# Two attention blocks on one core: the first block's output projection by a two-level product scheme, and who forms its factors

## The chip, the cores and the metric

One core of a Trainium2 chip runs the whole program. The metric is the time on the device in microseconds, as the median of several runs. All data is 32-bit floating point (`F32`).

## What is computed

The input holds B = 8 images of C = 512 channels and 32 x 32 = 1024 positions (tokens). Two attention blocks follow each other. The first has 32 normalisation groups and 8 heads:

```python
h = group_norm(x, gn_weight, gn_bias)
qkv = jnp.einsum('oc,bct->bot', w_qkv, h.reshape(B, C, T)) + b_qkv[None, :, None]
...
weight = jnp.einsum('bct,bcs->bts', q * scale, k * scale)
weight = jax.nn.softmax(weight.astype(jnp.float32), axis=-1).astype(weight.dtype)
a = jnp.einsum('bts,bcs->bct', weight, v)
out = jnp.einsum('oc,bct->bot', w_proj, a) + b_proj[None, :, None]
return x + out.reshape(B, C, H, W)
```

The second has 8 groups and one head over all 512 channels, with the same shape: normalisation, `q`, `k`, `v`, softmax, a projection, and the residual `x + ...`. This document is about the line `out = ...` and the residual behind it in the first block.

## The kernel before

**Images and stages.** A channel tile is 128 channels x 1024 tokens, so an image has four. The loop `for b in range(B)` (L1055 on) runs image b through the first block and image b - 1 through the second: attention of b (`attention0`), the projection of b (`projection`), then for image b - 1 the product `g` (`conv2("m", ...)`), the scores (`scores1`), the product `z` and the values (`values1`), and then `v`, `k` and `q` of image b + 1. The first image's start is in `prologue`. TensorE's instructions are kept in program order. So are VectorE's, GpSimd's and ScalarE's where the code says `tc.keep_in_program_order`; a scheduler places the others when the program is built. On the chip each engine takes its queue in order.

**Seven products in place of eight.** Every 512 x 512 by 512 x 1024 product is cut into halves each way, and formed with seven half-size products in place of eight (Strassen's scheme in Winograd's form). The seven left and seven right factors are the quarters themselves and sums of quarters. `image_factors` makes the right ones from four tiles: `t1 = b12 - b11`, `t2 = b22 - t1`, a new `b12 = b22 - b12`, and `t4 = b21 - t2` (two operations of 128 x 512 each, L1071 when pinned to VectorE). Factor 1 is b11, 2 is b21, 3 is b22, 4 is t4, 5 is t1, 6 is t2, 7 is the new b12.

**One level or two.** `by_channel` (through `wino`) stops there: 28 matmuls of 128 x 512. `conv2` does it twice: each of the seven factors is cut again by `inner_factors` (four subtractions of 128 x 256 for each factor, L414, on GpSimd), which gives 49 matmuls of 128 x 256. `conv2` takes the outer products in four parts (`pair`), one or two at a time, and goes through the seven inner products of a part in `inner_steps` in the order 1, 6, 2, 5, 7, with 3 and 4 left in `tail`, which the next part runs behind its product 1. After product 1 ScalarE copies its result to a second bank of PSUM, where 6, 7 and 4 go on. `add` (VectorE) and `nc.scalar.copy` bring results out; `more` (GpSimd, L535) adds one block of the output to another.

**Before, the projection uses `by_channel`** (L986), with the order `middle=(5, 6, 7, 2)`. VectorE's `residual` adds the projection's result and the bias `obias[0]` to `x` straight from PSUM (L964, L968, L970). The `x` tiles are loaded before the projection begins, and spilled behind it. The inner factors of `h`, which the next product `g` (or, in the first turn, `v`) reads, are 28 GpSimd operations in one run behind attention.

**Attention of the first block** goes through eight stretches of one pair of heads and half of the tokens. In a stretch ScalarE forms eight tiles of exponentials `e` (L651), VectorE adds them up (`sum`, L653 and L655), and TensorE multiplies them by `v` into `av`. Every two stretches (singly in the last two) `reciprocals` sums over partitions on TensorE (`sums`), copies the line to SBUF (L610), sends it through DRAM into 128 partitions, takes reciprocals (`recs`, L617) and spreads them back as `r`. The last stretch takes a short way: the reciprocal directly from PSUM (L607), and its DMAs from ScalarE's queue (L608, L628). Then `a` is scaled by `r` (L684). The lists `extra` put other work into the stretches: entry 2i + 1 of it comes behind the scaling in stretch i.

**SyncE's queue** issues nearly all loads in order. Weight factors are kept in DRAM (`keep`, or `keep2` with the second level) and loaded through three buffers in the order of the list `uses`. Image tiles and exponentials share one pool, `big`, of `NBIG` buffers of 4 KB in each partition.

Of the kernel before, what the change touches and what calls it, by code (L numbers as in the profile page):

```python
# [9 lines left out]
F32 = mybir.dt.float32  # L10
# [8 lines left out]
NBIG = 32  # L19
# [10 lines left out]
def two_attention_blocks_kernel(  # L30
# [22 lines left out]
    ident = const.tile([P, P], F32, name="ident")  # L53
    make_identity(nc, ident)
    ones = const.tile([P, P], F32, name="ones")
# [115 lines left out]
    def main_path(ctx):  # L171
# [100 lines left out]
        def weight_factors(t):  # L272
            return {p: t[:, ORDER.index(p), :, :] for p in range(1, 8)}

        def prepare(n):
            t = wpool.tile([P, 7, 2, C // 2], F32, tag="w", name=f"prepare_{n}")
            half = lambda kh, mh: weights[n][ts(kh, C // 2), ts(mh, C // 2)].rearrange("(k p) m -> p k m", p=P)
            f = weight_factors(t)
# [13 lines left out]
        wdram2 = {n: dram.tile([P, 7, 7, P], F32, name=f"sums2_{n}") for n in "qkmv"}  # L292
# [21 lines left out]
        uses = ["p", *layer0] if B > 1 else ["p"]  # L314
        for b in range(1, B):
            uses += ["p", *twice["m"], "z"] + (layer0 if b + 1 < B else [])
# [86 lines left out]
        def inner_factors(hf, uid, pin=lambda ins: ins):  # L403

            f, steps = {}, []
            for p in ORDER:
# [5 lines left out]
                def make(ops=((t1, b12, b11), (t2, b22, t1), (t3, b22, b12), (t4, b21, t2))):  # L412
                    for dst, x, y in ops:
                        pin(nc.gpsimd.tensor_tensor(dst, x, y, ALU.subtract))  # L414
# [86 lines left out]
        def conv2(n, f, bias, name, hooks=(), after=(), by_tokens=False):  # L501
# [30 lines left out]
            def more(dst, x, y, r, cc):  # L532

                (d,), (x,), (y,) = (blocks([at], r, cc) for at in (dst, x, y))
                nc.gpsimd.tensor_tensor(d, x, y, ALU.add)  # L535
# [8 lines left out]
            def pair(s, products, y, x, final):  # L544
# [6 lines left out]
                w = weights2[s // 2][:, (0, 2, 0, 1)[s] :]  # L551

                def mm(ps, j, start):
                    for i, p in enumerate(products):
                        wt = w[:, i, j - 1, :]
# [9 lines left out]
                def extra(r, cc, read, done):  # L565
                    if products == (7,):
                        if read:
                            more((0, 1), (0, 1), (1, 1), r, cc)
                        if done:
                            more((1, 1), (1, 0), (1, 1), r, cc)  # L570

# [6 lines left out]
            pair(0, (1, 5), [(1, 0), (1, 1)], None, [])  # L578
            pair(1, (2, 6), [(0, 0), (0, 1)], [(1, 0), (1, 0)], [load_weight, lambda: biased_half(0, 0)])
# [6 lines left out]
        def reciprocals(totals, uid, across, direct=None):  # L586
# [8 lines left out]
            for t in range(n):  # L595
                for i in range(4):
                    matmul(
                        sums[ts(i, 32), t, :, :], ones[:, :32], totals[t][:, :, ts(i, P)],
# [209 lines left out]

        def natural(wt, nm, banks):
# [3 lines left out]
            for kc in range(KC):  # L813
                for o in range(KC):
                    transpose(pt[o][:, ts(kc, P)], wt[kc][:, ts(o, P)], ident)
# [36 lines left out]
        def prologue():  # L852
            raw_k = raw("k", 5)
# [46 lines left out]
            for n in "pz":  # L900
                t, steps = prepare(n)
                later.append(steps)
                later.append([lambda n=n, t=t: keep(n, t), load_weight])
# [50 lines left out]
        def projection(b, af, xt, hooks=()):  # L954

            norm = GroupNorm(1, f"1_{b}", pinned=b > 0)
            stats, rest = [], []

            def residual(i, r, c, ps, u):
                oc = 2 * r + i  # L960
                xh = xt[oc][:, ts(c, HT)]

                tc.keep_in_program_order(
                    nc.vector.scalar_tensor_tensor(xh, ps, obias[0][:, oc : oc + 1], xh, ALU.add, ALU.add)  # L964
                )
                if (r, c) == (1, 1):

                    rest.append(lambda: tc.keep_in_program_order(nc.vector.tensor_add(xh, xh, u)))  # L968
                elif u is not None:
                    nc.vector.tensor_add(xh, xh, u)  # L970
                stats.append(lambda: norm.half_stats(oc, c, xh))

                if c == 1 - r:
                    stats.append(lambda: norm.end_stats(oc))

            def add_rest():
                for f in rest:
                    f()

            def store():  # L980
# [3 lines left out]

            by_channel(
                weight("p"), af, f"p_{b}", residual, middle=(5, 6, 7, 2), hooks=[[], [], hooks, [], [add_rest]],  # L986
                after=[load_weight, store],
            )
            return norm, stats
# [33 lines left out]
        def layer1_scores(b, inner):  # L1023
            g = conv2("m", inner, ubias, f"g1_{b}")
# [30 lines left out]
        for b in range(B):  # L1055
# [7 lines left out]
            elif B > 1:  # L1063
# [9 lines left out]

            if b > 0:
                hf, t = image_factors(h, f"h1_{b - 1}", here)
                for i, fs in enumerate((t[:1], t[1:2], (t[2], t[4]), (t[6], t[3]), (t[5], t[7]), steps[:2], steps[2:4])):
                    extra[2 * i + 3] += fs
            elif B > 1:
                hf, t = image_factors(h, "h0_1", here)
                for i, fs in enumerate((t[:2], (t[2], t[4]), (t[6], t[3]), (t[5], t[7], *steps[:2]), steps[2:4])):  # L1080
                    extra[2 * i + 7] += fs
            psum_pools(f"attention_{b}", 1)
            scaled = attention0(b, q, k, v, a, extra)
            if B > 1:
                for f in steps[4:7]:
                    f()
            psum_pools(f"products_{b}", 2)
            xt = [load_x(b, c, "x") for c in range(KC)]
            if B > 1:

                inner, sums2 = inner_factors(hf, f"h1_{b - 1}" if b > 0 else "h0_1", tc.keep_in_program_order)
                for f in sums2:
                    f()
                norm1, stats = projection(b, af, xt, [scaled, steps[7]])
# [235 lines left out]
```

## Time and profile before

| what | before |
|---|---|
| median of 3 runs (lowest, highest) | 2827.73 us (2827.01, 2831.14) |
| the profiled execution, its span on the core | 2828.69 us, 2826.9 us |
| granted TensorE clock, mean | 0.999 |
| DMA | 292.41 MB, 103 GB/s on average |
| projection's matmul records, `psa_p`, `psb_p`, `psc_p` | 448 of 128 x 512 |

PE is TensorE's matmul queue and PEld its weight loads; DVE is VectorE, ACT ScalarE, POOL GpSimd, SP SyncE, and a q behind a name is that engine's queue of DMA issues. A timeline line gives the start, the time from the start of its first to the end of its last instruction, the engine, the line of the code, the operation, output and inputs with their shape, and how many instructions it merges. In brackets it has the idle time of the engine just before, and what ended it. Durations overlap: the next instruction of an engine may start before the last has ended. Each 32-bit matmul shows as two records.

### The profile page before, as it was taken

The page shows a single profiled execution, that of the slowest core. Times are in us where ns is not written, and L with a number is a line of the kernel's source. Part 1 is how long each engine was busy: PE and PEld are TensorE (multiplying, and loading weights), DVE is VectorE, ACT ScalarE, POOL GpSimd, SP SyncE. Part 2 cuts the span into 40 slices and gives each one's busy share as a digit, 9 for nine tenths or more (in the row PEclk, how much of TensorE's full clock was granted, in tenths as well). Part 3 has the DMA queues.
Part 4 walks back from the last instruction along what each step waited for, and adds up shares of the span by engine and source line. Part 5 has one row for each costly group of instructions (what it writes and reads, how often), then busy time and mean ns, then how long its engine had stood idle before and what let it go on. Part 6 is the DMA issues. An engine that isn't in the chain of part 4 may idle for free.

```text
span 2826.9 us, 33696 instructions
## 1 busy us (share of the span) xinstructions
PE 2808.6 (99%) x12434; PEld 1693.5 (60%) x12434; DVE 2005.0 (71%) x2833; ACT 942.7 (33%) x1205; POOL 1099.4 (39%) x1131
## 2 busy tenths in 40 slices
PE   9999999999999999999999999999999999999998
PEld 5435735866367653677537674376843868338584
DVE  5478677776777767777677766777667776676765
ACT  1252452214522145221552215422154312633130
POOL 2204205841057410664107730177202672036672
PEclk9999999999999999999999999999999999999999
DMA  8634303043031330323212232123311224112301
GB/s 285 209 114 151 147 17 127 27 174 139 24 139 52 147 129 17 139 98 120 110 50 105 101 138 90 53 102 122 140 67 53 102 112 159 36 58 90 119 5 72
DMA packets 107344, 292.41 MB, mean 103 GB/s; under 512 B 19171, under 2 KB 51235, under 8 KB 97446
## 3 DMA queue, kind: packets, MB, share of 16 engines
q1 hardware_dynamic: 105382, 287.92, 28.8%
q10 hardware_dynamic: 1792, 2.29, 0.3%
q8 instruction: 100, 1.64, 0.2%
q14 instruction: 70, 0.57, 0.1%
HBM read 237.47 MB, written 52.70 MB: 103 GB/s over the span
## 4 chain that ended last, share of the span: by engine, by line
PE 96%; DVE 2%; issue 1%; DMA 0%; POOL 0%; ACT 0%; DVEq 0%; ACTq 0%; POOLq 0%
PE sc L62 16%; PE av L62 15%; PE psb_av L62 6%; PE psb L62 5%; PE psa_av L62 4%; PE psc_av L62 4%; PE psc L62 3%; PE psa L62 3%; PE psb_z L62 3%; PE psb_k L62 3%; PE psb_g L62 3%; PE psb_v L62 3%; PE psb_p L62 3%; PE psb_q L62 2%; PE psa_z L62 2%; PE psc_z L62 2%
## 5 line engine op out<-in xcount | busy, mean ns | idle before, releaser
L655 DVE TENSOR_TENSOR sum<-sum,e 128x1024 f32<-128x1024 f32 x384 | 483.9, 1260 | 37.4 <-ACT e L651 0.5
L651 ACT ACTIVATE e<-sc 128x1024 f32<-128x1024 f32 x512 | 476.0, 1054 | 75.8 <-PE sc L62 74.2
L62 PE MATMUL sc<-q,k 64*128 64x512 f32 x2048 | 456.8, 596 | 0.0
L62 PE MATMUL av<-e,v 128*64 128x512 f32 x2048 | 453.6, 595 | 0.0
L684 POOL TENSOR_TENSOR a<-a,r 128x512 f32<-128x512 f32 (+1 forms) x11 | 20.0, 1817 | 903.3 <-DMA r<-all_rows 771.0
L62 PEld LDWEIGHTS sc<-q,k 64*128 64x128 f32 x2048 | 191.6, 186 | 248.0 <-issue 110.6
L62 PEld LDWEIGHTS av<-e,v 128*64 128x64 f32 x2048 | 141.3, 137 | 304.4 <-issue 292.3
L653 DVE TENSOR_TENSOR sum<-e,e 128x1024 f32<-128x1024 f32 x64 | 78.4, 1225 | 166.5 <-ACT e L651 166.5
L669 ACT COPY a<-av 128x512 f32<-128x512 f32 x64 | 37.5, 586 | 321.9 <-PE av L62 321.9
L62 PE MATMUL psb<-inner,inner_h 128*128 128x256 f32 x448 | 116.1, 382 | 0.9
L62 PE MATMUL psa_av<-e,z 128*128 128x512 f32 x256 | 113.3, 595 | 0.0
L414 POOL TENSOR_TENSOR inner_h<-h,inner_h 128x256 f32<-128x256 f32 x120 | 111.6, 931 | 3.5
L135 ACT ACTIVATE h<-h,b,s 128x1024 f32<-128x1024 f32 x62 | 78.5, 1270 | 87.1 <-DMA h<-in_x 69.4
L414 POOL TENSOR_TENSOR inner_h<-h 128x256 f32<-128x256 f32 x60 | 64.6, 1076 | 83.6 <-ACT h L135 83.6
L62 PEld LDWEIGHTS psb<-inner,inner_h 128*128 128x128 f32 x448 | 83.9, 190 | 16.6 <-POOL inner L429 3.5
L462 ACT COPY psb_v<-psa_v 128x512 f32<-128x512 f32 (+1 forms) x28 | 14.5, 517 | 222.4 <-DVE o L785 141.5
L725 POOL TENSOR_TENSOR sum<-sum,e 128x1024 f32<-128x1024 f32 x32 | 76.1, 2378 | 27.4 <-ACT e L721 26.1
L62 PE MATMUL psb_g<-inner_h,w_m 128*128 128x256 f32 x336 | 86.0, 383 | 0.3
L414 POOL TENSOR_TENSOR inner_h<-t_h,inner_h 128x256 f32<-128x256 f32 x90 | 84.2, 935 | 2.4
L414 POOL TENSOR_TENSOR inner_h<-t_h 128x256 f32<-128x256 f32 x90 | 79.9, 894 | 9.7 <-DVE t_h L165 9.7
L62 PEld LDWEIGHTS psa_av<-e,z 128*128 128x128 f32 x256 | 48.0, 190 | 57.3 <-issue 56.6
L721 ACT ACTIVATE e<-e 128x1024 f32<-128x1024 f32 x64 | 65.8, 1053 | 48.5 <-DVE e L711 26.2
(358 smaller groups left out, 5574.8 us busy)
## 6 DMA issues: line engine op xcount, KB each, us to landing
x<-in_x SPq DMA_DIRECT2D x36, 512.0 KB
h<-in_x SPq DMA_DIRECT2D x32, 512.0 KB
r<-all_rows SPq DMA_DIRECT2D x64, 256.0 KB
spill<-x SPq DMA_DIRECT2D x32, 512.0 KB
h<-spill SPq DMA_DIRECT2D x32, 512.0 KB
x<-spill SPq DMA_DIRECT2D x32, 512.0 KB
out<-x SPq DMA_DIRECT2D x64, 256.0 KB
w_p<-sums_p SPq DMA_DIRECT2D x8, 1792.0 KB
```

What stands on the lines that cost most here:

```text
L62: tc.keep_in_program_order(nc.tensor.matmul(*args, **kw))
L135: tc.keep_in_program_order(nc.scalar.activation(dst, src, AF.Identity, bias=b, scale=s))
L414: pin(nc.gpsimd.tensor_tensor(dst, x, y, ALU.subtract))
L462: nc.scalar.copy(ps["b"], ps["a"])
L651: nc.scalar.activation(e, sc, AF.Exp, scale=(C // 8) ** -0.5)
L653: nc.vector.tensor_add(total, es[0], e)
L655: nc.vector.tensor_add(total, total, e)
L669: nc.scalar.copy(dst, av)
L684: engine.tensor_tensor(dst, dst, r, ALU.mult)
L721: nc.scalar.activation(e[c, cc, r], e[c, cc, r], AF.Exp, scale=scale)
L725: on = lambda dst, x, y: lambda: tc.keep_in_program_order(nc.gpsimd.tensor_tensor(dst, x, y, ALU.add))
```

## The change

The projection goes through `conv2` with a new flag `late`: two levels, and the outer products in the order `LATE`, in parts (1, 5), (6), (7, 3), (2, 4). With the flag, `more` is VectorE's. Its weight factors are prepared and stored with `keep2` in that order, and loaded in two parts (`uses`).

The attention output `a` gets inner factors of its own. For images 1 to 7 VectorE forms those of h for 1, 5 and 2 and of a for 1 and 5 in attention, and those of a and h for 6 behind it; GpSimd forms 3, 7, 2 and 4 of a, and 7, 3 and 4 of h, behind it. For image 0 GpSimd forms a's 1 and 5 in the seventh stretch, and VectorE h's 1, 5, 2 and 6 behind attention. The first two operations `t_a` move to one stretch earlier in images 1 to 7.

The residual is no longer added from PSUM. The `x` tiles are loaded when the projection has been issued, ScalarE adds the bias to them, and VectorE and GpSimd add the projection's halves, as hooks of the product that follows; the spill comes behind. `ident` moves to the pool `big`, `ones` shrinks, and `NBIG` goes from 32 to 34.

```diff
+LATE = (1, 5, 6, 7, 3, 2, 4)
-NBIG = 32
+NBIG = 34
...
-        uses = ["p", *layer0] if B > 1 else ["p"]
+        uses = [*twice["p"], *layer0]
         for b in range(1, B):
-            uses += ["p", *twice["m"], "z"] + (layer0 if b + 1 < B else [])
+            uses += [*twice["p"], *twice["m"], "z"] + (layer0 if b + 1 < B else [])
...
-                def make(ops=((t1, b12, b11), (t2, b22, t1), (t3, b22, b12), (t4, b21, t2))):
+                def make(engine=nc.gpsimd, ops=((t1, b12, b11), (t2, b22, t1), (t3, b22, b12), (t4, b21, t2))):
                     for dst, x, y in ops:
-                        pin(nc.gpsimd.tensor_tensor(dst, x, y, ALU.subtract))
+                        pin(engine.tensor_tensor(dst, x, y, ALU.subtract))
...
-                nc.gpsimd.tensor_tensor(d, x, y, ALU.add)
+                (nc.vector if late else nc.gpsimd).tensor_tensor(d, x, y, ALU.add)
...
+                    if products == (7, 3) and done:
+                        more((0, 1), (0, 1), (1, 1), r, cc)
+                        more((1, 1), (0, 0), (1, 1), r, cc)
...
             pair(0, (1, 5), [(1, 0), (1, 1)], None, [])
+            if late:
+
+                pair(1, (6,), [(0, 1)], [(1, 0)], [])
+                weights2.append(weight_part((n, 1)))
+                pair(2, (7, 3), [(0, 0), (0, 1)], [(0, 1), (0, 1)], [load_weight])
+                pair(3, (2, 4), [(1, 0), (0, 0)], [(1, 0), (0, 0)], [load_weight, *after])
+                return out
...
-        def projection(b, af, xt, hooks=()):
+        def projection(b, inner, hooks):
 
             norm = GroupNorm(1, f"1_{b}", pinned=b > 0)
-            stats, rest = [], []
...
+            y = conv2("p", inner, None, f"p_{b}", hooks, late=True)
+            xt = [load_x(b, c, "x") for c in range(KC)]
+
+            def biases():
+                for c in range(KC):
+                    nc.scalar.activation(xt[c], xt[c], AF.Identity, bias=obias[0][:, c : c + 1])
+
+            def residual(oc, c):
+                i, r = divmod(oc, 2)
+                yh = y[2 * (i if c else 1 - i) + r][:, ts(c, HT)]
                 xh = xt[oc][:, ts(c, HT)]
...
+                (nc.gpsimd if i else nc.vector).tensor_tensor(xh, xh, yh, ALU.add)
...
+            sums = [lambda oc=oc, c=c: residual(oc, c) for c in (1, 0) for oc in (2, 3, 0, 1)]
+            return norm, stats, [[biases], sums[:4], sums[4:], [store]]
...
             if b > 0:
-                hf, t = image_factors(h, f"h1_{b - 1}", here)
-                for i, fs in enumerate((t[:1], t[1:2], (t[2], t[4]), (t[6], t[3]), (t[5], t[7]), steps[:2], steps[2:4])):
-                    extra[2 * i + 3] += fs
...
+                plan = {
+                    3: t[:1], 5: [t[1], factor(ih, 1, V)], 7: [t[2], t[4]], 9: [t[6], t[3], factor(ih, 5, V)],
+                    11: [t[5], t[7], *steps[:2]], 13: [factor(ih, 2, V), factor(ia, 1, V), factor(ia, 5, V)], 15: steps[2:4],
+                }
+                first, last = [factor(ih, 6, V)], [factor(ih, p, G) for p in (7, 3, 4)]
+            else:
+                plan = {
+                    7: t[:2], 9: [t[2], t[4]], 11: [t[6], t[3]],
+                    13: [t[5], t[7], *steps[:2], factor(ia, 1, G), factor(ia, 5, G)], 15: steps[2:4],
+                }
+                first, last = [factor(ih, p, V) for p in (1, 5, 2, 6)], [factor(ih, p, G) for p in (7, 3, 4)]
...
             scaled = attention0(b, q, k, v, a, extra)
-            if B > 1:
-                for f in steps[4:7]:
-                    f()
+            for f in (steps[4], steps[5], factor(ia, 6, V), steps[6], factor(ia, 3, G), factor(ia, 7, G), *first):
+                f()
             psum_pools(f"products_{b}", 2)
...
+            norm1, stats, sums = projection(
+                b, inner_a, [[], [scaled, steps[7], factor(ia, 2, G), factor(ia, 4, G), *last]]
+            )
             if b > 0:
-                gf, gsteps = layer1_scores(b - 1, inner)
+                gf, gsteps = layer1_scores(b - 1, inner, sums)
```

## What I predicted before the run

> **What bounds the kernel.** I read the page first (busy shares, chain), then the timeline of TensorE over one projection, then VectorE, GpSimd and ScalarE around the same moment. The image shown is b = 2; images 1 to 7 repeat it every 345 us or so.
>
> ```profile
> span 2826.9 us, 33696 instructions
> PE 2808.6 (99%) x12434; PEld 1693.5 (60%) x12434; DVE 2005.0 (71%) x2833; ACT 942.7 (33%) x1205; POOL 1099.4 (39%) x1131
> PE 96%; DVE 2%; issue 1%; DMA 0%; POOL 0%; ACT 0%; DVEq 0%; ACTq 0%; POOLq 0%
> ```
>
> TensorE has work all the time and is the chain. So a removed product counts in full, and so does every wait that is put into its queue: there is no slack to hide one.
>
> ```profile
> 796.16 3.60 PE L62 MATMUL psc_p<-t_a,w_p 128*128 128x512 f32 x8
> 799.59 3.60 PE L62 MATMUL psb_p<-t_a,w_p 128*128 128x512 f32 x8
> ...
> 824.53 0.59 PE L62 MATMUL psa_g<-h,w_m 128*128 128x256 f32 x2
> 824.96 0.59 PE L62 MATMUL psa_g<-t_h,w_m 128*128 128x256 f32 x2
> ```
>
> Starts, not durations, give the rate: 8 records of 512 columns in 3.43 us, 0.429 each; 2 of 256 columns in 0.43, 0.216 each. A matmul is two records, so half the columns cost half the time.
>
> Next VectorE as that attention ends. Its first line is the scaling of the third channel tile, then come `t_a` (differences for the projection), the copy of the row sums that starts the reciprocal's DMA chain, and the last stretch's sum of eight exponentials with the reciprocal `recs` in its middle:
>
> ```profile
> 775.58 1.22 DVE L684 TENSOR_TENSOR a<-a,r 128x1024 f32<-128x1024 f32 x1
> 776.71 1.29 DVE L1071 TENSOR_TENSOR t_a<-a 128x512 f32<-128x512 f32 x2
> 778.10 0.42 DVE L610 COPY line<-sums 128x256 f32<-128x256 f32 x1
> 781.11 1.23 DVE L653 TENSOR_TENSOR sum<-e,e 128x1024 f32<-128x1024 f32 x1 [2.58 <-ACT e L651]
> 782.25 0.20 DVE L617 RECIPROCAL recs<-cols 128x8 f32<-128x8 f32 x1
> 782.44 3.88 DVE L655 TENSOR_TENSOR sum<-sum,e 128x1024 f32<-128x1024 f32 x3
> 786.80 5.11 DVE L655 TENSOR_TENSOR sum<-sum,e 128x1024 f32<-128x1024 f32 x3 [0.47 <-ACT e L651]
> 791.83 2.34 DVE L1071 TENSOR_TENSOR t_a<-a,t_a 128x512 f32<-128x512 f32 x2
> 794.09 1.75 DVE L607 RECIPROCAL line<-sums 128x256 f32<-128x256 f32 x1
> 795.76 2.16 DVE L1071 TENSOR_TENSOR a<-a,a 128x512 f32<-128x512 f32 x2
> ```
>
> The sum ends at 791.9. TensorE begins the matmul `sums`, which reads it, at 792.05. So VectorE is 0.14 us from holding TensorE up here. Image 0 shows what a later copy does, because there four `t` operations already stand ahead of it:
>
> ```profile
> 224.26 0.41 DVE L610 COPY line<-sums 128x256 f32<-128x256 f32 x1
> 227.91 0.20 DVE L617 RECIPROCAL recs<-cols 128x8 f32<-128x8 f32 x1 [1.47 <-DMA cols<-rows]
> ...
> 237.28 0.64 PE L62 MATMUL sums<-sum,ones 128*32 128x256 f32 x8 [1.05 <-DVE sum L655]
> ```
>
> From the end of the copy (224.67) two DMAs take 3.24 us; `recs` waits for them in VectorE's queue with six sums behind it, and TensorE waits 1.05 us.
>
> Two more views price what runs side by side, and ScalarE's queue:
>
> ```profile
> 793.58 1.17 POOL L414 TENSOR_TENSOR inner_h<-h,inner_h 128x256 f32<-128x256 f32 x1
> 794.72 0.72 POOL L414 TENSOR_TENSOR inner_h<-t_h 128x256 f32<-128x256 f32 x1
> ...
> 795.87 0.58 ACTq L608 DMA_DIRECT2D all_rows<-line  x1
> 797.69 1.12 ACTq L628 DMA_DIRECT2D r<-all_rows  x2
> ```
>
> GpSimd's 128x256 takes 0.72 alone (0.69 start to start) and 1.17 beside VectorE; VectorE's two 128x512 take 1.29 alone (776.71) and 2.34 beside GpSimd (791.83). So one of each pass together in about 1.14 = 0.60 + 0.69 - 0.15. The trace has no VectorE 128x256 with both inputs in SBUF. With one in PSUM (L530) it takes 0.42 alone and 0.76 for two, so 0.33 start to start; 0.50 where it needs the one before (the sums: 1.31 apart, 1.23 long, so 0.08 over the length). A factor of four operations is then 0.33 + 0.50 + 0.33 + 0.33 = 1.5 us alone. Beside GpSimd I estimate one at 0.33 + 0.69 - 0.15 = 0.87.
>
> **Removed.** The projection's 28 products of 512 columns (56 records x 0.429 = 24.04 us) become 49 of 256 (98 x 0.216 = 21.20). TensorE is spared 2.84 us an image, 22.7 in all.
>
> **Added at `sums`: 1.9 us, images 1 to 7.** In VectorE's new order the inner factors h2, a1 and a5, twelve operations, stand between the scaling and the copy. `t_a` has moved a stretch earlier, where VectorE waits 1.67 us anyway. From 776.71 they take 3 x 1.5 = 4.5, so the copy runs at 781.2 to 781.6, and `recs` at 781.6 + 3.24 = 784.85 in place of 782.25: 2.6 later. The 0.47 of idle and 0.14 of slack go against it: 1.9 to 2.0. Bounds 1.4 (every operation 0.33) and 2.6 (each 0.40). Image 0's row gives the same: copy to `sums` 13.0 us, so 794.2, 2.1 late. The factors h1 and h5, 1.5 us each, fall in stretches where VectorE waits 3.15 and 2.54 us for ScalarE: nothing.
>
> **Added at the first product: 0.9 us.** The new routine copies product 1 to a second bank (L462, 0.57 us) before product 6 may go on there. Elsewhere the tail of the routine before it fills the gap (`psa_g` at 809.89 goes ahead of 16 `psb_p` and `psc_p` records). Here the pools change and no tail is left: 0.57 and about 0.3 for both hops; 0.8 to 1.0.
>
> **Added in the first half-pair: 4.3 us.** TensorE goes through the inner products 1, 6, 2, 5, 7, then product 1 of the next part, then 3 and 4 (0.865 each for two outer factors). Product 4 goes into the bank that VectorE must first have read (the add behind 7). Before that add VectorE's queue holds, counted from the end of the sum: two t2 beside GpSimd 2.34; the reciprocal 1.66 (1.75 less the 0.09 by which starts overlap); two b12 differences 1.2 (GpSimd has nothing to do until they are there); inner a6, four beside GpSimd's a7, 3.5; t4 0.6; inner h6 1.5; the add with its hop 0.77. Sum 11.5. TensorE needs 0.1 + 0.57 (`sums`) + 0.9 + 6.5 x 0.865 = 7.2 to get there. It waits 4.3. ScalarE explains the first 1.5 of it: the copy that product 3 needs stands behind the `r` DMAs, which wait 1.8 us for the row to land (795.87 to 797.69). Bounds: VectorE alone throughout 8.4, so with ScalarE's queue 1.4; every SBUF operation beside GpSimd 15.0, so 7.8.
>
> **Added in the later pairs: 1.5 us.** From that add to the one that lets the last part's product 7 go, VectorE has five operations of 512 columns and sixteen of 256 (5 x 0.60 + 16 x 0.33 = 8.3), and eight extra SBUF additions, which used to be GpSimd's in such a routine: 2.6 alone, 7.0 beside GpSimd, so 10.9 to 15.3. TensorE's work over the same stretch is fifteen steps of 0.865, 13.0. GpSimd has twenty inner operations there, so the upper end is nearer (2.3), less what falls between its waits: 1.5; 0 to 4.
>
> **At nothing.** The second load of `w_p` adds 1.3 MB an image; both parts are asked for before attention. Two of the four `x` loads now queue on SyncE behind the load of `w_m`'s second part, which waits for the projection; at the 360 to 400 GB/s seen at 816 the third lands some 7 us later, about when ScalarE comes to its bias: 0, at most 1 (in the upper end above). Residual adds and statistics go to the next stage, where VectorE waits for TensorE; the mean is wanted only two stages on. GpSimd's factors a7, a3 and those of h end 8 us or more before they are read, a2 and a4, which wait for the last scaled tile, 2 to 3 us. If that cover were gone, each would cost at most its length, 3 us. Preparing `w_p` adds four GpSimd operations of 2.08 us (L308) in the first attention, where GpSimd is idle.
>
> **Image 0.** It has four times h on VectorE behind attention in place of one (about 4 us more ahead of the add), and eight GpSimd operations beside the last sums (1.5, 0 to 3). Net: -2.8 + 1.5 + 0.9 + 8 + 1.5 = +9; 3 to 18.
>
> **Sum.** An image 1 to 7: -2.8 + 1.9 + 0.9 + 4.3 + 1.5 = +5.8 (bounds +0.8 and +12.6). Seven: +40.6, image 0 +9: +49.6. The profiled execution took 2828.69 us (span 2826.9), 1 us over the median 2827.73, so it is typical and I add to the median: 2877.
>
> The trace weighs the shared time of VectorE and GpSimd at 1.14 us for a pair. The Trainium skill (SBUF — State Buffer, Who interferes with whom) says that a VectorE instruction with two SBUF inputs and a GpSimd one that reads SBUF block each other for the whole instruction. By that rule a 128x256 beside GpSimd would cost 0.33 + 0.69 = 1.02; ten such an image, 0.15 more each, would bring the total to about 2889.
>
> TensorE waited 3.62 us once in this trace, at its start, and the granted clock behind it reads 1.00. The Trainium skill (TensorE: Matmul & The Clock Gate, Why this matters for your kernels) warns that idle gaps above some 3 us drop it to half clock. Were the 4.3 us wait to do that for one of the page's windows of 3.4 us, an image would lose 1.7 more (an estimate from the page), and the total would be 2891.
>
> **Rivals.** *Faster:* VectorE keeps up, and only the 0.9 us gap is left: 8 x (0.9 - 2.84) = -15.5, 2812. For it: VectorE is 71% busy, and GpSimd's 28 operations no longer run into the projection's start. Against it: the queue order, the 0.14 us of slack, and image 0's row. It decides if the last sum ends within 0.9 us of today's and the first add less than 8 us behind it. *Cover without contention:* GpSimd and VectorE hardly meet, all lower bounds hold: 7 x 0.8 + 3 = +9, 2836. *Pile-up:* the upper bounds: 7 x 12.6 + 18 = +106, 2934. That the products are not removed can be excluded: the changed program holds 49 per projection.
>
> **Chances.** Forecast 0.67, its own range 2845 to 2910; no contention 0.17, of which 0.06 within 0.2% (5.7 us, about what a measurement can tell from no change); faster 0.10; pile-up 0.06. So slower 0.84, same 0.06, faster 0.10. The range 2828 to 2910 leaves out the faster case and the pile-up.
>
> **What would show it.** Right: TensorE's share falls to some 97%; `sums` waits for VectorE's sum about 2 us in each image; records of the projection wait for a VectorE add, 2 to 3 us, and for ScalarE copies; 98 records of 0.216 each. Wrong: no wait at `sums`, or the first add right behind product 7.

## The result, and the profile after

The changed kernel takes 2943.46 us (median of four runs, 2934.75 to 2956.41), the kernel before in the same comparison 2827.57. The ratio is 1.0411, 95% interval 1.037 to 1.0451: slower by 116 us. I had said 2877, slower by 49.6. The sign was right; the size was not, and the range missed it.

The profiled execution is the fastest of the four, 2934.75 us (span 2932.8), 106 us over that of before. Traces explain these 106. First the page: busy shares and the chain.

```profile
span 2932.8 us, 35003 instructions
PE 2836.1 (97%) x12770; PEld 1779.2 (61%) x12770; DVE 2161.1 (74%) x3241; ACT 1002.1 (34%) x1285; POOL 1162.4 (40%) x1175
PE 80%; DVE 14%; issue 3%; DMA 2%; ACT 0%; POOL 0%; SPq 0%; DVEq 0%; ACTq 0%; POOLq 0%
```

VectorE had 2% of the chain and now has 14%. TensorE is busy 27.5 us longer although 22.7 us of products were removed; part of its work ran at a lower clock. What TensorE waited for (total, times, longest):

```profile
PE sums L61 <- DVE sum L665: 28.8, 10, 8.6
PE psb_p L61 <- DVE u_p L529: 20.2, 8, 2.5
PE psb_p L61 <- DVE p L529: 14.8, 7, 3.2
PE psb_p L61 <- ACT psb_p L461: 6.0, 9, 0.8
PE psb_v L61 <- DVE v L529: 4.0, 1, 4.0
```

The same image as in the prediction, b = 2, on TensorE's timeline:

```profile
839.05 0.64 PE L61 MATMUL sums<-sum,ones 128*32 128x256 f32 x8 [2.24 <-DVE sum L665]
...
842.25 2.07 PE L61 MATMUL psb_p<-inner_a,w_p 128*128 128x256 f32 x4 [0.71 <-ACT psb_p L461]
...
850.78 1.56 PE L61 MATMUL psb_p<-inner_a,w_p 128*128 128x256 f32 x6 [1.36 <-DVE p L529]
...
867.09 2.06 PE L61 MATMUL psb_p<-inner_a,w_p 128*128 128x256 f32 x4 [2.53 <-DVE u_p L529]
868.95 1.06 PE L61 MATMUL psa_g<-h,w_m 128*128 128x256 f32 x2
```

All four forecast waits are there, in their forecast places: at `sums`, at the first product 6, at product 4 of the first half-pair (a half-pair is one of the four parts that `conv2` goes through), and at the last product 7. Four records of 256 columns take 2.07 and 2.06 at 842 and 867; at 847 four take 1.03. The stretches of this image with their granted clock (columns: busy time of PE, PEld, DVE, ACT, POOL, then PEclk, and the DMA engines' busy share and GB/s):

```profile
836.40:839.80 3.40, 1.16 (x11) 0.34 (x10) 3.29 (x3) 0.58 (x1) 3.32 (x3) 1.00 0.00 0
839.80:846.60 6.80, 6.08 (x14) 4.37 (x15) 6.77 (x9) 1.69 (x3) 4.95 (x6) 0.50 0.45 170
...
863.70:867.10 3.40, 0.87 (x5) 0.41 (x4) 3.40 (x8) 0.00 (x0) 3.32 (x5) 1.00 0.98 407
867.10:870.50 3.40, 3.40 (x8) 2.75 (x9) 2.57 (x7) 0.00 (x0) 2.96 (x5) 0.50 0.59 240
```

Behind the 2.24 us wait TensorE runs 6.8 us at half clock, behind the 2.53 us wait 3.4 us. Over the whole program the clock record has 98.4 us at 0.50, 6.2 of it at the program's end, where the kernel before has it too.

VectorE in the same image: the copy, `recs` and the last sum; the inner factor a6 beside GpSimd; the first add; two of the eight extra additions; the operation that lets the last product 7 go.

```profile
825.79 0.41 DVE L620 COPY line<-sums 128x256 f32<-128x256 f32 x1
...
829.47 0.20 DVE L627 RECIPROCAL recs<-cols 128x8 f32<-128x8 f32 x1 [2.14 <-DMA cols<-rows]
...
832.56 6.43 DVE L665 TENSOR_TENSOR sum<-sum,e 128x1024 f32<-128x1024 f32 x4 [0.46 <-DVE sum L665]
...
843.99 0.94 DVE L413 TENSOR_TENSOR inner_a<-t_a 128x256 f32<-128x256 f32 x1
844.97 0.83 DVE L413 TENSOR_TENSOR inner_a<-t_a,inner_a 128x256 f32<-128x256 f32 x1
...
850.04 0.68 DVE L529 TENSOR_TENSOR p<-psb_p,c_p 128x512 f32<-128x512 f32 x1
...
860.75 1.80 DVE L534 TENSOR_TENSOR p<-p,p 128x256 f32<-128x256 f32 x2
...
866.62 0.41 DVE L529 TENSOR_TENSOR u_p<-psb_p,p 128x256 f32<-128x256 f32 x1
```

Image 0 is where most of the surprise is. VectorE's timeline in its attention:

```profile
141.62 11.27 DVE L665 TENSOR_TENSOR sum<-sum,e 128x1024 f32<-128x1024 f32 x6
...
178.51 0.25 DVE L627 RECIPROCAL recs<-cols 128x16 f32<-128x16 f32 x1 [13.76 <-DMA cols<-rows]
```

and TensorE's waits there and in the next stage:

```profile
152.95 0.64 PE L61 MATMUL sums<-sum,ones 128*32 128x256 f32 x8 [2.97 <-DVE sum L665]
192.60 1.08 PE L61 MATMUL sums<-sum,ones 128*32 128x256 f32 x8 [8.57 <-DVE sum L665]
256.66 1.08 PE L61 MATMUL sums<-sum,ones 128*32 128x256 f32 x8 [2.85 <-DVE sum L665]
...
301.07 3.40 PE L61 MATMUL psb_v<-w_v,inner_h 128*128 128x128 f32 x16 [4.00 <-DVE v L529]
```

Six such sums take 7.87 where GpSimd is idle; 11.27 is beside the preparation of `w_p`. The first reciprocal's `cols` came 13.76 us after VectorE was ready for it, 4.90 in the trace of before.

A table from the first records of each stage in the traces (us; attention from its first `sc` record to the projection's first, "to g" from there to the first `psa_g`, both as means; the rows from e1_filled on are experiments of the next section):

| | first projection starts | attention, images 1 to 7 | to g, images 1 to 7 | p of image 1 to p of image 7 |
|---|---|---|---|---|
| before | 237.8 | 116.82 | 17.27 | 2072.1 |
| changed | 257.7 | 119.01 | 29.75 | 2135.9 |
| e1_filled | 257.7 | 118.84 | 28.46 | 2135.7 |
| e2_slots | 256.8 | 117.85 | 27.22 | 2110.7 |
| e3_more | 257.6 | 119.04 | 25.96 | 2109.4 |
| e6_a6 | 258.0 | 119.02 | 28.87 | 2134.4 |
| e8_spread | 253.3 | 116.83 | 21.84 | 2076.4 |
| e11_x0 | 244.4 | 116.86 | 20.92 | 2066.8 |

"To g" holds 40 of 56 projection records before (40 x 0.429 = 17.2) and 90 of 98 after (90 x 0.216 = 19.4). So the changed kernel loses 29.75 - 19.4 = 10.3 us an image there, 2.2 in attention, and 0.8 behind g's start (that stretch should be 16 x 0.429 - 8 x 0.216 = 5.1 shorter and is 4.3): 13.3 less the 2.84 saved, 10.5 for each of images 1 to 7, 73 in all. Prologue and image 0 lose the other 33.

### The profile page after: what moved, and what is told of

It is laid out like the page before. It is cut to its first block, busy times and chain, and to the rows that moved or that the text cites. A ratio compares the mean times of both kernels' runs of the same rounds, so it can differ in the third digit from the quotient of the medians.

```text
span 2932.8 us, 35003 instructions
## 1 busy us (share of the span) xinstructions
PE 2836.1 (97%) x12770; PEld 1779.2 (61%) x12770; DVE 2161.1 (74%) x3241; ACT 1002.1 (34%) x1285; POOL 1162.4 (40%) x1175
## 4 chain that ended last, share of the span: by engine, by line
PE 80%; DVE 14%; issue 3%; DMA 2%; ACT 0%; POOL 0%; SPq 0%; DVEq 0%; ACTq 0%; POOLq 0%
PE sc L61 12%; PE av L61 11%; PE psb_av L61 5%; PE psb L61 5%; DVE sum L665 4%; PE psc_av L61 4%; PE psa_av L61 3%; PE psc L61 3%; PE psa L61 3%; PE psb_z L61 3%; PE psb_k L61 3%; PE psb_g L61 3%; PE psb_q L61 2%; PE psb_v L61 2%; PE psa_z L61 2%
## 5 line engine op out<-in xcount | busy, mean ns | idle before, releaser
L61 PE MATMUL psb_p<-inner_a,w_p 128*128 128x256 f32 x336 | 102.7, 437 | 41.7 <-DVE u_p L529 20.2
L61 PEld LDWEIGHTS psb_p<-inner_a,w_p 128*128 128x128 f32 x336 | 67.8, 213 | 68.2 <-DVE u_p L529 23.4
L735 POOL TENSOR_TENSOR sum<-sum,e 128x1024 f32<-128x1024 f32 x32 | 76.1, 2378 | 28.7 <-ACT e L731 27.5
L726 POOL TENSOR_TENSOR e<-e,e 128x512 f32<-128x512 f32 x64 | 80.4, 1271 | 11.5 <-DVE e L721 11.5
L61 PE MATMUL psb_v<-w_v,inner_h 128*128 128x128 f32 x588 | 78.6, 280 | 4.2 <-DVE v L529 4.0
```

What stands on the lines that cost most here:

```text
L61: tc.keep_in_program_order(nc.tensor.matmul(*args, **kw))
L726: nc.gpsimd.tensor_tensor(blocks(dst, r, cc)[0], blocks(x, r, cc)[0], blocks(y, r, cc)[0], ALU.add)
L735: on = lambda dst, x, y: lambda: tc.keep_in_program_order(nc.gpsimd.tensor_tensor(dst, x, y, ALU.add))
```

## Experiments

**Is it the clock?** Theory: the half-clock stretches are what I left out. Rival: they are a symptom, and VectorE's queue sets the time.

```diff
+            for _ in range(3 if fill else 0):
+                matmul(sums[:, 0], fill[0][:, :P], fill[1][:, : 2 * P], start=True, stop=True, skip_group_check=True)
...
+            fills = {(0, 6): 1, (0, 4): 6, (3, 7): 4}
...
+                def fill(j):
+                    for _ in range(fills.get((s, j), 0) if late else 0):
+                        matmul(spare[:, : 2 * P], w[0][:, 0, :], f[products[0]][1], start=True, stop=True, skip_group_check=True)
```

> The changed kernel with idle TensorE time filled: spare products of 128x256 (their results go to a spare bank and are not used) stand in TensorE's queue ahead of the places where it waited: 3 ahead of the last `sums` of each image, 1 ahead of the first product 6, 6 ahead of product 4 of the first half-pair, 4 ahead of product 7 of the last (0.43 us each at full clock). The changed kernel's trace has 92 us at a granted clock of 0.50 besides the end of the program, 75 of them behind these places. Theory A (VectorE's queue bounds the projection, and the half clock costs only where TensorE and not VectorE is late): the half-clock stretches behind these waits go, but the first one of an image saves nothing, since VectorE's add behind product 7 comes no earlier; only the stretch behind the late wait does, 1.7 us an image: 8 to 16 us off the changed kernel's 2943, so 2927 to 2935, mean granted clock above 0.995. Theory B (the half clock itself is what was missed): half of 75, 37 us off, 2906. Theory C (only waits count): no gain, 2943 or a little more.

Measured: 2940.29 (2930.18 to 2943.26), ratio to before 1.039 (1.0366 to 1.0413). Its cores' view:

```profile
core 0: 2936.3 us, clock 0.996
```

The mean granted clock rose from 0.984 to 0.996, half-clock time fell from 98 to 26 us, and the time fell by 3, which the runs' own spread covers. Image 2 on TensorE, without its half-clock stretches:

```profile
840.99 0.64 PE L61 MATMUL sums<-sum,ones 128*32 128x256 f32 x8 [1.57 <-DVE sum L674]
...
849.99 2.75 PE L61 MATMUL spare_p<-a,w_p 128*128 128x256 f32 x12
852.73 1.56 PE L61 MATMUL psb_p<-inner_a,w_p 128*128 128x256 f32 x6
...
869.04 1.13 PE L61 MATMUL psb_p<-inner_a,w_p 128*128 128x256 f32 x4 [0.81 <-DVE u_p L530]
870.01 0.59 PE L61 MATMUL psa_g<-h,w_m 128*128 128x256 f32 x2
```

From the start of `sums` to the last product 7 there are 28.05 us here (869.04 - 840.99) and 28.04 in the changed kernel (867.09 - 839.05), at half clock or not. VectorE's queue sets this stretch. Only what stands behind it gained: `psa_g` starts 29.02 after `sums` in place of 29.90. Over the seven images "to g" is 1.3 shorter, but just behind the start of g TensorE now waits for VectorE, 1.22 us in each of them:

```profile
873.12 1.13 PE L61 MATMUL psb_p<-inner_a,w_p 128*128 128x256 f32 x4 [1.22 <-DVE p L530]
```

Theory B fell. Image 2 shows what A says of the first stretch; in the total A's 8 to 16 us are not found, and it lies nearer to C, no gain.

**Half clock where TensorE is the bound.** The kernel before, with a later copy:

```diff
-                    extra[2 * i + 3] += fs
+                    extra[2 * i + 3] += fs * (4 if i == 5 else 1)
```

> The kernel before with nothing but a later row-sum copy: the first two differences of a are computed four times instead of once (six more VectorE operations of 0.60 us ahead of the last `line` copy in images 1 to 7). The last sum should end some 2.4 us later (3.6 less the idle 0.47, 0.14 and what the DMA wait takes up). In this kernel VectorE waits for TensorE behind attention, so nothing hides a half clock there. Theory A (half clock costs where TensorE is the bound): the wait at `sums`, 2.4, and at least one window of 3.41 us at 0.50 behind it, 1.7: 4.1 an image, 29 in all, 2857. Theory C (only the wait counts): 7 x 2.4 = 17, 2845, granted clock 1.00. In images where the wait falls across two windows of the clock's grid, A gives the wait alone, so down to 2850.

Measured: 2849.93 (2846.81 to 2854.09), 1.0082 (1.0065 to 1.0099), 21 us slower. `sums` waits 1.93 to 2.99 us in the seven images, 16.2 together. Only one wait is followed by half clock, the 2.38 of image 3; the longest, 2.99 in image 5, is not. Two windows of each:

```profile
1140.80:1144.20 3.40, 1.01 (x8) 0.16 (x8) 3.30 (x3) 0.58 (x1) 2.75 (x2) 1.00 0.96 369
1144.20:1147.60 3.40, 3.40 (x11) 1.18 (x4) 3.40 (x3) 0.00 (x0) 3.32 (x5) 0.50 0.54 220
1837.10:1840.50 3.40, 2.28 (x12) 0.54 (x8) 3.09 (x4) 0.59 (x1) 1.41 (x1) 1.00 0.81 251
1840.50:1843.90 3.40, 1.53 (x11) 0.65 (x12) 3.40 (x3) 0.00 (x0) 3.32 (x3) 1.00 0.97 395
```

In the first row TensorE idles 3.40 - 1.01 = 2.39, in the last two 1.12 and 1.87. Span against span: 2845.0 - 2826.9 = 18.1 = 16.2 of waits + 1.7 for one window at half speed, and little else. Between the two theories, nearer to C: here half clock costs its full price, but in the profiled execution it came once in seven. The other three runs are 3 to 7 us longer at a mean clock of 0.996 or 0.997 against 0.999, so there it may have come more often; they have no trace.

**VectorE's factors ahead of the copy and behind attention.** Three factors of h moved to stretches with idle time:

```diff
-  5: [t[1], factor(ih, 1, V)], 7: [t[2], t[4]], 9: [t[6], t[3], factor(ih, 5, V)],
-  11: [t[5], t[7], *steps[:2]], 13: [factor(ih, 2, V), factor(ia, 1, V), factor(ia, 5, V)],
+  5: [t[1], factor(ih, 1, V)], 7: [t[2], t[4], factor(ih, 5, V)], 9: [t[6], t[3], factor(ih, 2, V)],
+  11: [t[5], t[7], *steps[:2], factor(ih, 6, V)], 13: [factor(ia, 1, V), factor(ia, 5, V)],
-  first, last = [factor(ih, 6, V)], [factor(ih, p, G) for p in (7, 3, 4)]
+  first, last = [], [factor(ih, p, G) for p in (7, 3, 4)]
```

> The changed kernel with three VectorE factors of h elsewhere in images 1 to 7: h5 a stretch earlier, h2 from the last stretch but one to the stretch before h5's old place, h6 from behind attention into the stretch of the first differences of a. These stretches have 1.7 to 4.0 us of VectorE idle time each. Theory A: `sums` does not wait any more (2.2 us less an image), the first add comes 1.5 us earlier, one half-clock stretch an image goes; 3.5 to 5 us an image, 25 to 35 off 2943: 2908 to 2918. Rival (the time behind attention is set by something else than VectorE's queue: ScalarE's copies or GpSimd's factors): `sums` gains its 2.2, and the waits behind it grow by as much: 2935 to 2943.

Measured: 2916.81 (2908.6 to 2925.9), 1.0323 (1.0301 to 1.0346), 27 off, as theory A said: 1.2 an image in attention and 2.5 before g. Some 1.0 of wait at `sums` is left, where A had none.

**The extra additions.**

```diff
-  (nc.vector if late else nc.gpsimd).tensor_tensor(d, x, y, ALU.add)
+  tc.keep_in_program_order(nc.gpsimd.tensor_tensor(d, x, y, ALU.add))
-  [[], [scaled, steps[7], factor(ia, 2, G), factor(ia, 4, G), *last]]
+  [[], [scaled, steps[7], factor(ia, 2, G), factor(ia, 4, G)], [], last]
```

> The changed kernel with the eight extra additions of the third half-pair on GpSimd, and GpSimd's factors h7, h3, h4 behind them (after the last half-pair's product 7). In the changed kernel VectorE spends 5.9 us on them in image 2 (0.61 to 1.80 a row at L534). Theory A: the late wait for u_p (2.5 us) and the half-clock stretch behind it (1.7) go: 4 us an image, 25 to 32 off 2943: 2911 to 2918. Rival (GpSimd is the one that is late then: the last half-pair's write of the first quarter has to wait for its reads): a wait of 2 us or more for GpSimd in its place, 2935 to 2950.

Measured: 2911.37 (2905.39 to 2920.32), 1.0304 (1.0287 to 1.0321), 32 off. The wait for `u_p` is gone from the list of waits, and "to g" is 3.8 us shorter. GpSimd does the eight in 5.98 us and nobody waits for them. VectorE's first add and last `u_p` and GpSimd's eight, in image 3:

```profile
1197.11 0.69 DVE L529 TENSOR_TENSOR p<-psb_p,c_p 128x512 f32<-128x512 f32 x1
...
1209.63 0.76 DVE L529 TENSOR_TENSOR u_p<-psb_p,p 128x256 f32<-128x256 f32 x2
...
1207.38 5.98 POOL L534 TENSOR_TENSOR p<-p,p 128x256 f32<-128x256 f32 x8
```

From that add to the end of the last `u_p` VectorE takes 13.3 us in place of 17.0. This is one of two causes of about the same size: from image 1's attention to the end of the program this run gains 31 us, e2_slots 30. The run makes two edits at once, since GpSimd's factors of h move too. VectorE's other operations in the stretch got no cheaper (10.0 us of work against 9.5), so the gain is the additions, 5.5 us of its queue. How much of these 5.5 is their own length and how much the factors beside them, no run separates.

**a6 to GpSimd.**

```diff
-  (steps[4], steps[5], factor(ia, 6, V), steps[6], factor(ia, 3, G), factor(ia, 7, G), *first)
+  (factor(ia, 3, G), factor(ia, 6, G), steps[4], steps[5], steps[6], factor(ia, 7, G), *first)
```

> The changed kernel with the inner factor a6 on GpSimd (behind a3) instead of VectorE in images 0 to 7; all else as in the changed kernel. In image 2 VectorE spends 3.46 us on a6 beside GpSimd (843.99 to 847.45), with the first add behind it at 850.04. Theory A (VectorE's queue between the last sum and the first add sets the first half-pair's end): the add comes 3.5 us earlier, the wait for it goes and 2 to 3.5 us an image with it; later VectorE work follows earlier as well: 2917 to 2930. Rival (GpSimd then delivers a6, needed by product 6 of the second half-pair, 2 us or more too late, or its contention slows VectorE by as much): 2938 to 2950.

Measured: 2936.99 (2932.14 to 2941.81), 1.0383 (1.0365 to 1.04): 6 off, which the spread could hold, and nearly what the rival said. The 3.46 us of a6 left VectorE, but GpSimd now works longer beside it, and the operations behind pay:

```profile
847.11 2.16 DVE L1076 TENSOR_TENSOR a<-a,a 128x512 f32<-128x512 f32 x2
849.19 1.21 DVE L1076 TENSOR_TENSOR t_a<-a,t_a 128x512 f32<-128x512 f32 x1
850.32 0.94 DVE L413 TENSOR_TENSOR inner_h<-t_h 128x256 f32<-128x256 f32 x1
```

The two differences take 2.16 (1.22 in the changed kernel), h6's operations up to 0.94 each (0.42). The first add comes 10.48 us behind `sums` in place of 10.99.

**Image 0: the queue in front of the reciprocal.** e4_image0 moved one load in the program, but the scheduler issued it where it had been, between `rows` and `cols`:

```diff
-                load_weight,
             ])
+            later.extend([[], [], [load_weight]])
```

> The changed kernel with the load of the first part of w_v in image 0 three slots later, so that in SyncE's queue it no longer stands between the first reciprocal's `rows` and `cols`. In the changed kernel VectorE waits 13.76 us for `cols` there (4.90 before the change), TensorE 8.57 us at `sums`, and three windows of half clock follow. Theory A (queue order): that wait goes to 2 us or less, `sums` gains 8 us and the half-clock windows go: 9 to 14 us off 2943, 2929 to 2934. Rival (the DMA engines are full with the 3.1 MB of w_p's store and loads, whatever the order): `cols` lands as late, at most 3 us off, 2940 to 2943.

Measured: 2943.43 (2935.48 to 2946.99), 1.0397 (1.038 to 1.0415). It decides nothing on the queue and serves as a repeat of the changed kernel. With the load held in program order behind the reciprocal:

> The same question as e4_image0, whose kernel still issued w_v's load between `rows` and `cols` (SyncE's queue had the same order as before the edit): now the load is held in program order, and stands behind the first reciprocal's four DMAs. Theory A (queue order): VectorE's wait of 13.4 us for `cols` goes to some 5 us or less (4.90 before the change), the wait of 8.3 us at `sums` and the half-clock windows behind it go: 9 to 14 us off 2943, 2929 to 2934. Rival (the DMA engines are full with w_p's store and loads, so `rows` and `cols` land late whatever the queue's order): at most 3 us off, 2940 to 2943.

Measured: 2934.09 (2931.46 to 2940.09), 1.0381 (1.0364 to 1.0399): 9 off, of which the traces show 3.3 (the first projection starts at 254.4 in place of 257.7); the rest lies within the runs' spread. The wait for `cols` fell from 13.76 to 10.73, the one at `sums` from 8.57 to 5.57. Half an answer: `rows` is issued at 156.24 and `cols`, which waits for it, only at 170.08, with 4.9 MB of `w_p` and `sums_z` issued just ahead. That these hold it up is tested in e10_first0.

```profile
154.91 0.81 SPq L327 DMA_DIRECT2D w_p<-sums_p  x2
155.76 0.43 SPq L288 DMA_DIRECT2D sums_z<-prepare_z  x1
156.24 0.61 SPq L624 DMA_DIRECT2D rows<-line  x1
170.08 0.31 SPq L627 DMA_DIRECT2D cols<-rows  x1
```

**All placements together, then the rest of image 0.** e8_spread puts one factor in each stretch, a6 and the additions on GpSimd, e4b's load behind the reciprocal, and in image 0 h1 and h5 into attention and h2 and h6 on GpSimd.

```diff
...
+  3: [t[0], factor(ih, 1, V)], 5: [t[1], factor(ih, 5, V)], 7: [t[2], t[4], factor(ih, 2, V)], 9: [t[6], t[3], factor(ih, 6, V)],
+  11: [t[5], t[7], *steps[:2], factor(ia, 1, V)], 13: [factor(ia, 5, V)], 15: steps[2:4],
...
```

> All placements together: in images 1 to 7 VectorE's factors spread one to a stretch (h1, h5, h2, h6 in the four stretches from the second on, a1 in the sixth, a5 alone in the seventh), a6 on GpSimd, the eight extra additions on GpSimd with h7, h3, h4 behind them; in image 0 h1 and h5 in attention, h2 and h6 on GpSimd, and w_v's load behind the first reciprocal. Theory A: TensorE becomes the bound of the projection again, with the 0.7 us gap at the first product left: 0.7 - 2.84 = -2 us an image against the kernel before for images 1 to 7, image 0 still 10 to 20 slower (prologue 1.4, contention with the preparation of w_p 3, its half clock): 2824 to 2835. Theory B' (another wait takes the place, GpSimd's 28 factors and 8 additions being its candidate): 2 to 5 us an image more, 2838 to 2865.

Measured: 2857.92 (2854.02 to 2861.61), 1.0106 (1.0089 to 1.0123). Attention of images 1 to 7 is back at 116.83, and image 1 to image 7 takes 2076.4, 4.3 over before. Image 1's attention starts at 354.5 (330.4 before the change), so image 0 and the prologue cost 24 where A had 10 to 20. The larger miss is in images 1 to 7: 4 us slower together where A had 14 faster. That is rival B', a new wait in place of the old ones, though not for GpSimd: in image 2 TensorE waits twice for ScalarE's copies, at the first products 6 and 3, and A had counted one.

```profile
818.71 1.13 PE L61 MATMUL psb_p<-inner_a,w_p 128*128 128x256 f32 x4 [0.72 <-ACT psb_p L463]
...
823.69 0.70 PE L61 MATMUL psc_p<-a,w_p 128*128 128x256 f32 x2 [0.73 <-ACT c_p L453]
```

The two do not make up the whole difference; the rest has no cause here.

Product 5 ahead of 6 in the first half-pair:

```diff
-            for j in (6, 2, 5, 7):
+            for j in (5, 6, 2, 7) if five else (6, 2, 5, 7):
```

> e8_spread with TensorE's inner products of the first half-pair in the order 1, 5, 6, 2, 7, 4 and 3 as before (in e8_spread 1, 6, 2, 5, 7): product 5 needs a bank of its own and no copy, so it covers ScalarE's copy that product 6 waits for (0.71 us an image), and ScalarE's copy of 5 gets ahead of the two DMA issues that product 3 waited behind (0.76). Theory A (TensorE is the bound of the projection there): both waits go, 1.4 us an image, 11 off 2858: 2845 to 2849. Rival (ScalarE's copies only change places, and product 7 or 4 waits instead): 2854 to 2858.

Measured: 2854.41 (2846.89 to 2855.66), 1.008 (1.0062 to 1.0099). 3.5 off, the rival's figure: product 7 now waits for ScalarE's copy `u_p` instead, 4.6 us over eight images.

e10_first0 adds z's store and the loads of `w_p` and `w_v` behind the reciprocals, and image 0's differences and a1, a5 one slot earlier:

```diff
-  later.append([lambda n=n, t=t, store=store: store(n, t), load_weight])
+  later.append([lambda n=n, t=t, store=store: store(n, t)])
...
+  late = lambda: load_weight(tc.keep_in_program_order)
+  later[4] = [*later[3], late, *later[4]]
+  later[3] = []
+  later.extend([[late], [], [], [late]])
```

> e9_five with image 0's first attention rearranged: z's store and the loads of w_p and w_v behind the first (and second) reciprocal in SyncE's queue, the differences of h one slot earlier, a1 and a5 one slot earlier on GpSimd. e8_spread waits 5.83 and 3.14 us at `sums` there, with some 4 us of half clock. Theory A (the reciprocal's 8 KB stand behind w_p's and z's megabytes in the DMA queues): the 5.8 goes to 1 or less, the 3.1 to 1 or less: 8 to 12 us off e9_five, 2834 to 2840. Rival (the loads then stand in the way of the second reciprocal): 3 us or less.

Measured: 2841.72 (2839.38 to 2845.24), 1.0044 (1.0029 to 1.0058): 12.7 off. `cols` is issued at 157.53, 1.8 us behind `rows`, and the first projection starts at 243.6 (254.5 in e9_five). Theory A, a little short of its figure; the seven stores of `w_p` still go ahead of `rows`, so it is the loads and z's store that had held `cols` up. How much of the 12.7 the moved operations add is not separated.

e11_x0 adds image 0's four x loads (`load`), in program order, ahead of `w_v`'s second part:

```diff
+            if b == 0:
+                hooks[1].append(load)
```

> e10_first0 with image 0's four loads of x, held in program order, ahead of the load of w_v's second part in SyncE's queue. In e8_spread that load waited for a weight buffer until 271.98, the x loads behind it landed some 10 us later, the biases and residual adds with them, and an add of the v stage stood behind them and behind the statistics in VectorE's queue: `psb_v` waited 7.41 us, with two windows of half clock behind it. Theory A (queue order on SyncE): 7 to 10 us off e10_first0, to 2825 to 2832. Rival (the DMA engines' rate bounds it, 400 GB/s over that stretch, or the residual adds are late anyhow): 0 to 3 us.

Measured: 2835.71 (2831.26 to 2842.9), 1.0027 (1.0017 to 1.0038): 6 off, a little under A; the two kernels' runs overlap, and by the traces image 1's attention starts 3.9 earlier. The same edit on the changed kernel alone:

> The changed kernel with that last edit alone (image 0's x loads ahead of w_v's second part). In the changed kernel `psb_v` waits 4.00 us in image 0's next stage, with one window of half clock behind it. Theory A: 4 to 6 us off 2943, 2937 to 2939. Rival: no gain that can be told from the changed kernel's own spread (2935 to 2956).

Measured: 2943.71 (2936.75 to 2947.12), 1.0409 (1.0391 to 1.0426): nothing. The x loads were issued at 255.55, ahead of `w_v`, and `psb_v` still waits 4.8 us: VectorE reaches the adds of that stage late, with residual adds and statistics ahead of them in its queue. The load order matters only once VectorE keeps up.

e11_x0 is 108 us faster than the changed kernel and still 0.27% slower than the one before. From image 1's projection to image 7's it takes 2066.8 us against 2072.1: 0.9 us an image are gained out of the 2.84. No version here is faster than the kernel before, since 9.7 us are still lost by the start of image 1's projection (456.9 against 447.2).

## Why the prediction was wrong, step by step

- **Removed, 2.84 us an image:** right. Where the clock is 1.00, pairs of records start 0.43 apart, as said.
- **At `sums`, 1.9:** attention is 2.2 longer on the mean of seven; image 2 waits 2.24. `recs` ran 829.47 - 826.20 = 3.27 us behind the copy's end; the row of before had given 3.24.
- **First product and first half-pair, 0.9 + 4.3 = 5.2:** image 2 takes 850.78 - 839.62 = 11.16 for 26 records worth 5.6, so 5.5. My count put the first add 11.5 us behind the sum; it ended at 11.7. The view shows waits of 0.71 and 1.36 only, because TensorE spent the rest at half clock, inside time it would have waited anyway. Operations beside GpSimd, estimated at 0.87, stand 0.87 apart in a6 (843.99 to 847.45, four of them); the 1.02 that the prediction also weighs does not fit.
- **Later pairs, 1.5:** this term failed. TensorE took 16.3 from product 4 (850.78) to product 7 (867.09) for 60 records worth 13.0: 3.3 lost. VectorE's queue needs as long, 16.3 from the end of the first add (850.72) to the end of the last `u_p` (867.03); counted from the add's start it is 17.0, and 17.0 in e1_filled and e2_slots too. Of the 16.3, 14.9 are work, within my bounds of 10.9 to 15.3 and near the upper one; 1.4 are waits for TensorE (1.06 and 0.32). I had taken 0.8 off the upper end for what falls between TensorE's waits, where 1.4 had to be added to VectorE's work: in a queue that is fed in small pieces, work and hand-overs add up. The eight additions are the part that made the queue too long: in e3_more, where GpSimd does them, the stretch takes 13.3.
- **Half clock, at nothing:** an omission, but a small one. I weighed it only behind the first half-pair's wait. It came behind the waits at `sums`, where it cost nothing, and at the last product 7, where it cost 1.0 before g in image 2 and, on the mean, some 0.8 behind. In e1_filled waits for VectorE took its place (1.22 us an image behind the start of g, 3.8 once at `psb_av`); the total moved by 3.
- **Image 0, 9, and "preparing `w_p`, loads of `w_p`" at nothing:** this failed most, 33 in place of 9. I looked at GpSimd, found it idle there, and stopped. The four operations ran beside VectorE's sums (7.87 became 11.27), and seven stores of `w_p`, its two loads and z's store entered the queue ahead of the 8 KB that the first reciprocal needs. e10_first0 shows that the loads and z's store delay it, e4b_image0 a part for `w_v`'s load; the effect of the preparation on VectorE is read from the trace only, as no run moved it.
- **Residual adds, at nothing:** right for images 1 to 7. In image 0 VectorE is late by then: 4.00 us at `psb_v`.

Added up for the profiled execution: images 1 to 7 lose 73 instead of 40.6, image 0 and the prologue 33 instead of 9. Of the rivals the pile-up (2934) came nearest in its number, by luck: its 106 are 88 for images 1 to 7 and 18 for image 0, where 73 and 33 came. In kind it holds for the later pairs and image 0 and not for the first half-pair, which ended near the forecast. (Its bound of 2.6 at `sums` is also a slip: twelve operations of 0.40 give 2.3.) *Faster* fell with the first wait at `sums`; *no contention* with a6's rows.

Two things stay open. TensorE's first wait, for a weight load in the prologue, is 1.1 us longer (4.7 instead of 3.6). It is 4.7 to 5.3 in every trace of the changed kernel and its variants, and 3.6 and 3.8 in the two without the change; no run tells why. And the changed kernel's four runs span 22 us, those of before 4; I have traces of only two of its kind.

At one place a rule and the trace differ. The Trainium skill (TensorE: Matmul & The Clock Gate, What's actually happening) has a free-running activity window of 3413 ns and half clock after an idle window. The window is here: all half-clock stretches of the changed kernel last 3.41, 6.83 or 10.24 us, but for the one that the program's end cuts off. But a window need not be idle. Summed over such windows, 1.98 us of idle time in one was followed by half clock (changed kernel, from 2614.8) and 1.90 was not (e1_filled, from 300.8). The line is not sharp by this measure: 1.89 was in e3_more (from 1184.2), 2.03 was not in e4_image0 (from 2655.0). And a wait of 3.23 us split over two (image 0, 271.65) left the clock at 1.00.

## What to carry to other kernels

Before pricing waits on the engine that waits, add up the whole queue of the engine it waits for, from one hand-over to the next, and price every two-input SBUF operation there at its cost beside the neighbour. Moving one operation to the neighbour may only move the contention to the next one. A preparation that grows brings more stores and loads: look at which small, urgent transfer they will stand in front of.

## What I had not expected of the hardware

Two to two and a half us of waiting are enough for half clock, or not, by where they fall: 2.38 us in one window cost a further 1.7 us, 2.99 over two windows nothing. And half clock can be free: in image 2, with none of its 6.8 us left, the stretch from `sums` to the last product 7 took 28.05 us instead of 28.04.
